# Four edits to a six-stage decoder kernel: product order in two fp8 attention stages, seven groups in the shared expert, and the last feed-forward's input built a block earlier

## The chip, the cores and the metric

The kernel runs on one core of one Trainium2 chip. The metric is the device time of one execution in microseconds (us); the number given for a kernel is the median over several executions. The engines are named as in the profile: PE (TensorE, matrix products), PEld (its weight loads), DVE (VectorE), ACT (ScalarE), POOL (GpSimd) and SP (SyncE, which issues most transfers). Each works through its own queue in order, and instructions wait on one another through semaphores.

## The reference

The reference is a pre-norm decoder of two layers over x of shape (16, 112, 512), that is 1792 tokens in 14 tiles of 128, with a context of shape (16, 375, 512). All is in f32 except where values are rounded to fp8. Six residual steps follow one another:

```
x = x + L0_attn(layernorm(x))                 # causal self attention, 16 heads of 32
x = x + L0_xattn(layernorm(x), ctx)           # fp8 self attention and fp8 cross attention, one output projection
x = x + L0_ffn(layernorm(x))                  # mixture of 8 experts, top 2, and a shared expert
x = x + L1_attn(layernorm(x))                 # causal self attention with biases
x = x + L1_xattn(layernorm(x), ctx)           # cross attention of one wide head
x = x + L1_ffn(layernorm(x))                  # SwiGLU with ternary weights, 512 -> 2048 -> 512
```

The parts that the change touches:

```
# L0_xattn: rows are scaled, clipped, rounded to bf16 and then to fp8; 16 query heads, 8 key heads of 128
q = _ln(linear(ln_out, wq), qln)      k = _ln(linear(ln_out, wk), kln)     v = linear(ln_out, wv)
kx, vx = split(cond @ w_kv_x.T)       kx = _ln(kx, kxln)
cat = concat(gqa(q, k, v), gqa(qx, kx, vx))
out = linear(fp8(cat / proj_smooth), wproj)
# L0_ffn, the shared expert, hidden size 448
out = silu(xf @ sw1) * (xf @ sw3) @ sw2
# L1_ffn
out = (silu(x @ wu.T) * (x @ wg.T)) @ wd.T
```

## The kernel before

The residual x stays on chip as 14 tiles of 128 tokens. The stages run one after another: first attention (to about 262 us of the span), fp8 self attention (262 to 900), fp8 cross attention (900 to 2247), the mixture of experts (2247 to 2786), the second layer's attention (2786 to 3104), its cross attention (3104 to 3458) and its feed-forward (3458 to the end).

**fp8 self attention.** `stage_fp8_self` works on four quarters of the heads (q = 0 to 3) times 16 batches. The list `order` holds these units; quarters 0 and 1 are interleaved, since quarter 0 waits for its inputs. The function `turn(n)` issues, in a fixed order, the pieces of several units at different depths: the projection of queries of unit n (`project_q`), the scores of unit n-2, the keys and values of unit n (`project_kv`, `ps_kv`), the values of unit n-3, the normalization of unit n (`normalize`, tile `qk`), the transposes of unit n-1, and the output of unit n-4. PE and ACT run in the order written; from turn 5 on DVE does too. POOL and SP, and DVE in turns -2 to 4, are ordered by the scheduler.

Units of quarter 0 that bring a new tile have a `Quantized` input: `load` fetches a normed row tile `xn`, `transpose` writes `ps_xt` on PE, `scale(count)` makes the bf16 tiles `y` on ACT from it (10 pieces in one turn, 6 in the next), `round_qk` rounds to fp8 for queries and keys (tile `xq`: four passes on DVE in `round_fp8`, then a subtraction on POOL), and `round_v` does so for values (tile `xv`). In the kernel before, an input for unit n is loaded at the end of turn n-3, transposed and scaled in turn n-2, and rounded in turn n-1, `round_v` near its end. Between them PE also runs 16 `early` products (`ps_early`, L697), one for each batch: the keys and values of the last third of the context for the first cross quarter, stored to DRAM. The dictionary `early` says how many stand at the start of each turn.

**fp8 cross attention.** `stage_fp8_cross` has again four quarters times 16 batches. A `CrossUnit` projects queries (`queries`, tile `qn`), then keys and values in three chunks of 125 context rows (`keys_values(ch)`, L1135, tiles `kn`, with one buffer, and `vn`). In the first quarter the third chunk needs no product: its result was made early and is loaded. Each chunk is normed at once by `normed`: squares on ACT, a sum on DVE (`cu_v`, L1111), an inverse root on POOL (L530, L531), a multiplication on DVE (L1113). `scores` computes the scores of two heads, their maximum (`ex_m`, L1078) and exponentials (L1079), the reciprocal, and the division of the probabilities (`pr`, L1170). `transpose_probs` (L1178), `values` (L1188) and `output` (L708, then x on DVE, L948) follow. In turn n the units n, n-1 and n-2 are mixed, and the scheduler orders the engines by that program.

**Shared expert.** In the mixture of experts, `shared_expert` returns a list of steps for a block of 4 or 3 tiles (512 or 384 tokens): four `up(f)`, each with two groups of four f32 products over 112 of the 448 hidden columns (L1444), a silu on ACT (L1447) and a product on DVE (`h`, L1448), and one `down(i)` per tile (L1455), four products each. Blocks 0 and 1 are computed around the routing of the tokens, blocks 2 and 3 at the end of the stage, beside the gathers of the experts' rows on POOL (`yg`, L1420), and ACT's reading of the feed-forward's weights (`w_sum`, L1776). An f32 product stands as two instructions in the trace.

**Last feed-forward.** `stage_ffn` goes through four blocks of 4, 4, 3 and 3 tiles. For each it takes the layer norm, transposes the rows (`ps_xt`, L1823) and splits them into two parts (`halves`, tile `xt`, L1804 on ACT and L1805 on DVE), and then runs 16 steps over the hidden columns, each with `ps_u` and `ps_g` (L1854) and the `down` of the step before (`ps_o`, L1836). `ps_u` and `ps_xt` share two banks.

Of the kernel before, what the change touches and what calls it, by code (L numbers as in the profile page):

```python
# [2 lines left out]

# [6 lines left out]
F32 = mybir.dt.float32  # L10
# [20 lines left out]
TILE_BLOCKS = ((0, 4), (4, 4), (8, 3), (11, 3))  # L31
E, HID = 8, 448
HC = 112
MOE_WIDTHS = (KC * HID, KC * HID, 4 * D)
MT = (2 * B * S + E * (P - 1)) // P
FQ = 4
# [927 lines left out]
def stage_fp8_self(k):  # L964
# [4 lines left out]
    with k.stage("s2a", mm=3, tr=1, sc=4) as wk:  # L969
# [36 lines left out]
        end = max(inputs)  # L1006

        def turn(n):
            new, half = inputs.get(n + 2), inputs.get(n + 1)
            products(early.get(n, 0))  # L1010
            if at(n):
                units[n].project_q(weights[order[n][0]], xq.pop(n))
            if at(n - 2):
                units[n - 2].scores()
            if at(n):
                units[n].query_sums()
            if half:
# [24 lines left out]
            if n >= last[1] and tiles and not loaded:  # L1042
                loaded.append((tiles[0], cross_input(k, wk, tiles.pop(0))))
            if at(n - 1):
                units[n - 1].transpose()
            if new:
                new.transpose()
                new.scale(10)
            elif at(n + 2):
# [32 lines left out]
class CrossUnit:  # L1082
# [3 lines left out]
    def __init__(self, k, wk, q, b, w, heads):  # L1086
        self.k, self.wk, self.q, self.b, self.w = k, wk, q, b, w
        self.heads, self.tile = heads, tile_of(b)
        if self.tile is not None:
            self.xq = wk.tile([P, KC, P], F32R, tag="xq", name="xq", bufs=2)  # L1090
            k.nc.sync.dma_start(out=self.xq.bitcast(F32), in_=k.xx_dram[self.tile])
        self.ct = ct = wk.tile([P, KC * SC + 12], F32, tag="ct", name="ct", bufs=2)
        if q == 0:
            n = SC - CC
            self.ct, self.early = chunks(ct, 0, KC, n), ct[:CC, KC * n :].rearrange(
                "p (h d) -> p h d", d=P
            )
            k.nc.sync.dma_start(out=self.ct, in_=k.a["ctx_t"][b][:, :, :n])
            k.last_load = k.nc.sync.dma_start(out=self.early, in_=k.kv_dram[b])
        else:  # L1100
            self.ct = chunks(ct, 0, KC, SC)
            k.last_load = k.nc.sync.dma_start(out=self.ct, in_=k.a["ctx_t"][b])
# [21 lines left out]
    def keys_values(self, ch):  # L1124
        k, wk, nc = self.k, self.wk, self.k.nc
        w = chunks(self.w.kv, 0, KC, 512)
        if ch == 0:
            self.kn = wk.tile([CC, NCH, 2, P], F32, tag="kn", name="kn", bufs=1)
            self.vn = wk.tile([CC, NCH, 2, P], F32, tag="vn", name="vn", bufs=2)
        if ch == NCH - 1 and self.q == 0:  # L1130
            pkv = self.early
        else:
            pkv = k.psum.tile([CC, 4, P], F32, tag="mm", name="ps_kv", bufs=3)
            for c in range(KC):
                nc.tensor.matmul(  # L1135
                    pkv, self.ct[:, c, ch * CC : (ch + 1) * CC], w[:, c, :],
                    start=c == 0, stop=c == KC - 1,
                )
# [17 lines left out]
    def scores(self, heads):  # L1156
# [10 lines left out]
        nc.vector.reciprocal(sums, sums)  # L1167
        for i, h in enumerate(heads):
            pr = self.pr[:, h, :]
            nc.vector.tensor_scalar(pr, pr, sums[:, i : i + 1], None, ALU.mult)  # L1170

    def transpose_probs(self):
        k, wk, nc = self.k, self.wk, self.k.nc
# [23 lines left out]
            add_output(self.k, t, self.heads.o.pop(t), self.w.get(1), "acc")  # L1197


def stage_fp8_cross(k):  # L1200


    with k.stage("s2b", mm=3, tr=2, sc=2, acc=1) as wk:
        units = []
        for n in range(4 * B + 2):
            q, b = divmod(n, B)
            new = last = None
            if q < 4:
                if b == 0:
                    w, heads = k.next_w, Heads()  # L1210
                new = CrossUnit(k, wk, q, b, w, heads)
                units.append(new)
                new.queries()
                new.keys_values(0)
            if 0 < n <= 4 * B:
                last = units[n - 1]
                last.scores((0, 1))
            if new:
                new.keys_values(1)
            if last:  # L1220
                last.scores((2, 3))
            if new:
                new.keys_values(2)

            first = new is None or q == 0
            if n > 1 and first:
# [12 lines left out]
                k.next_w.step(1)  # L1239
            if b == 2 and q == 3:  # L1240
                with behind(k):
                    k.weights["shared"] = load_pieces(k, "shared", k.a["shared_w"], MOE_WIDTHS)


def gates(k, wk, gw, xts):
# [185 lines left out]
def shared_expert(k, wk, xt, first, count):  # L1431

    nc, n = k.nc, count * P
    w1, w3, w2 = moe_weights(k.weights["shared"])
    tok = slice(first * P, first * P + n)
    hs = []

    def up(f):
        cols = slice(f * HC, (f + 1) * HC)
        p1 = k.psum.tile([HC, n], F32, tag="sc", name="ps_1", bufs=2)  # L1440
        p3 = k.psum.tile([HC, n], F32, tag="mm", name="ps_3", bufs=3)
        for pp, w in ((p1, w1), (p3, w3)):
            for c in range(KC):
                nc.tensor.matmul(pp, w[:, c, cols], xt[:, c, tok], start=c == 0, stop=c == 3)  # L1444
        sl = wk.tile([P, 4 * P], F32, tag="sl", name="sl", bufs=2)[:HC, :n]
        h = wk.tile([P, 4 * P], F32, tag="h", name="h", bufs=5)[:HC, :n]
        nc.scalar.activation(sl, p1, AF.Silu)  # L1447
        nc.vector.tensor_tensor(h, sl, p3, ALU.mult)  # L1448
        hs.append(h)

    def down(i):
        x = k.x[:, first + i, :]
        po = k.psum.tile([P, D], F32, tag="mm", name="ps_o", bufs=3)
        for f in range(4):
            nc.tensor.matmul(  # L1455
                po, hs[f][:, i * P : (i + 1) * P], w2[:, f, :], start=f == 0, stop=f == 3
            )
        nc.vector.tensor_tensor(x, x, po, ALU.add)

# [345 lines left out]
    k.nc.vector.tensor_tensor(lo, x, hi.bitcast(F32), ALU.subtract)  # L1805


def stage_ffn(k):
    nc, t = k.nc, k.ternary
    rows_out = k.out.rearrange("b s d -> (b s) d")  # L1810
    with k.stage("s6", mm=3, tr=2, sc=2, acc=1) as wk:
        todo = [(q, m) for q in (2, 3) for m in range(3)]
        for first, count in TILE_BLOCKS:
            nt = count * P
            rows = [k.x[:, first + i, :] for i in range(count)]
            xt = wk.tile([P, 2, KC, 4 * P], F32R, tag="xt", name="xt", bufs=2)[:, :, :, :nt]
            mv, rs = row_stats(k, rows)
            for i, r in enumerate(rows):
                xn = wk.tile([P, D], F32, tag="xn", name="xn", bufs=2)
                normalize(k, xn, r, mv, rs, i)  # L1820
                ps = k.psum.tile([P, KC, P], F32, tag="sc", name="ps_xt", bufs=2)
                for c in range(KC):
                    nc.tensor.transpose(ps[:, c, :], xn[:, c * P : (c + 1) * P], k.ident)  # L1823
                tok = slice(i * P, (i + 1) * P)
                halves(k, xt[:, 0, :, tok], xt[:, 1, :, tok], ps)
# [15 lines left out]
            for n in range(4 * FQ):  # L1841
# [93 lines left out]
def laid_out(i):  # L1935
# [70 lines left out]
    got["shared_w"] = expert_w(sw1, sw3, sw2)  # L2006
# [20 lines left out]
```

## Time and profile before

| what | us |
|---|---|
| median of 3 runs | 3805.27 (3802.48 to 3808.19) |
| the profiled execution | 3800.22 |
| its span | 3798.5 |
| PE busy in it | 3600.9 (95%) |
| DVE, ACT, POOL busy | 1785.3, 1429.4, 927.7 |
| mean granted PE clock | 0.983 |

All lines of the profile come from the one profiled execution, so sums over its rows are to be set against 3800.22, not against the median. The span leaves out 1.7 us around the program. A row of the timeline gives start, length, engine, line, operation and tiles, and in brackets the idle time just before it with what ended that. The granted clock is the rate that the PE had; at 0.5 a product takes about double.

### The profile page before, as it was taken

The page shows a single profiled execution, that of the slowest core. Times are in us where ns is not written, and L with a number is a line of the kernel's source. Part 1 is how long each engine was busy: PE and PEld are TensorE (multiplying, and loading weights), DVE is VectorE, ACT ScalarE, POOL GpSimd, SP SyncE. Part 2 cuts the span into 40 slices and gives each one's busy share as a digit, 9 for nine tenths or more (in the row PEclk, how much of TensorE's full clock was granted, in tenths as well). Part 3 has the DMA queues.
Part 4 walks back from the last instruction along what each step waited for, and adds up shares of the span by engine and source line. Part 5 has one row for each costly group of instructions (what it writes and reads, how often), then busy time and mean ns, then how long its engine had stood idle before and what let it go on. Part 6 is the DMA issues. An engine that isn't in the chain of part 4 may idle for free.

```text
span 3798.5 us, 46330 instructions
## 1 busy us (share of the span) xinstructions
PE 3600.9 (95%) x16482; PEld 2325.5 (61%) x16482; DVE 1785.3 (47%) x3888; ACT 1429.4 (38%) x4133; POOL 927.7 (24%) x1314
## 2 busy tenths in 40 slices
PE   7988899998999999999999999999989999999999
PEld 4545787886555566566666654555544445556788
DVE  5546777876445544544445542111243453224333
ACT  3546766554444444444444430111124431112222
POOL 2324555653222322322222210000132220000000
PEclk9999999999999999999999999999989999999999
DMA  2144333432211211211121114999830022222000
GB/s 84 58 140 142 114 111 122 151 118 73 62 55 63 66 50 47 74 47 52 44 82 44 49 40 145 319 318 317 297 117 12 1 78 76 74 80 76 12 12 17
DMA packets 118118, 364.56 MB, mean 96 GB/s; under 512 B 13280, under 2 KB 33248, under 8 KB 108848
## 3 DMA queue, kind: packets, MB, share of 16 engines
q1 hardware_dynamic: 105504, 332.20, 27.0%
q0 software_dynamic: 5040, 16.52, 1.2%
q10 hardware_dynamic: 7344, 12.89, 0.9%
q8 instruction: 131, 2.15, 0.2%
q14 instruction: 99, 0.81, 0.1%
HBM read 317.09 MB, written 44.47 MB: 95 GB/s over the span
## 4 chain that ended last, share of the span: by engine, by line
PE 69%; DVE 10%; POOL 5%; issue 3%; ACT 2%; DMA 2%; POOLq 0%; SPq 0%; ACTq 0%; DVEq 0%
PE ps_kv L1135 14%; PE ps L1492 6%; PE ps_av L1188 4%; PE ps_s L1163 3%; PE ps_y L1510 3%; PE ps_acc L708 3%; PE ps_q L708 3%; PE ps_u L1854 3%; PE ps_o L360 3%; PE ps_o L1836 3%; PE ps_g L1854 3%; PE ps_q L1605 3%; PE ps_p L1698 3%; PE ps_pt L1178 2%; PE ps_v L1620 1%
## 5 line engine op out<-in xcount | busy, mean ns | idle before, releaser
L1135 PE MATMUL ps_kv<-w_kv,ct 128*125 128x512 f32 x1408 | 637.6, 592 | 0.0
L1135 PEld LDWEIGHTS ps_kv<-w_kv,ct 128*125 128x125 f32 x1408 | 260.2, 187 | 276.1 <-issue 242.0
L549 POOL TENSOR_TENSOR r_o<-r_t,r_m 128x64 fp32r<-128x64 bf16 (+6 forms) x224 | 146.4, 670 | 331.4 <-DVE r_t L547 307.7
L1111 DVE TENSOR_REDUCE cu_v<-sq 125x2 f32<-125x256 f32 (+1 forms) x248 | 118.6, 478 | 215.7 <-ACT sq L1110 215.7
L1079 ACT ACTIVATE pr<-ps_s,ex_m 112x375 f32<-112x375 f32 (+1 forms) x272 | 157.4, 579 | 165.3 <-DVE ex_m L1078 154.9
L1492 PE MATMUL ps<-w_expert,xgt 128*128 128x448 f32 x560 | 216.4, 539 | 0.7 <-ACT xgt L1484 0.7
L530 POOL TENSOR_SCALAR cu_v<-cu_v 125x2 f32<-125x2 f32 (+1 forms) x248 | 48.0, 194 | 635.5 <-DVE cu_v L1111 633.2
L531 POOL TENSOR_TENSOR cu_v<-cu_v,mhalf 125x2 f32<-125x2 f32 (+1 forms) x248 | 190.0, 766 | 20.4
L236 POOL TENSOR_TENSOR pr<-pr,nq_s 112x448 f32<-112x448 f32 (+1 forms) x120 | 118.5, 988 | 296.1 <-DVE nq_s L235 243.7
L231 ACT ACTIVATE pr<-ps_s,nq_m 112x112 f32<-112x112 f32 (+1 forms) x480 | 166.9, 378 | 60.6 <-DVE nq_m L223 59.6
L1163 PE MATMUL ps_s<-kt,qt 128*112 128x375 f32 x512 | 183.6, 479 | 1.9 <-ACT pr L1079 1.4
L1078 DVE TENSOR_REDUCE ex_m<-ps_s 112x1 f32<-112x375 f32 (+1 forms) x272 | 148.1, 545 | 69.3 <-PE ps_s L1725 67.0
L1110 ACT ACTIVATE sq<-ps_kv 125x256 f32<-125x256 f32 x176 | 67.4, 383 | 272.4 <-PE ps_kv L1135 218.3
L524 ACT ACTIVATE qt<-ps_t,turned 128x448 f32<-128x448 f32 (+6 forms) x224 | 116.4, 581 | 131.3 <-PE ps_t L1147 122.5
L1188 PE MATMUL ps_av<-pt,vn 125*128 125x224 f32 x768 | 164.1, 363 | 0.0
L1492 PEld LDWEIGHTS ps<-w_expert,xgt 128*128 128x128 f32 x560 | 103.6, 190 | 92.0 <-issue 91.0
L1178 PEld LDWEIGHTS ps_pt<-ident,pr 112*125 112x125 f32 x768 | 104.0, 190 | 86.9 <-DVE pr L1170 49.1
L1188 PEld LDWEIGHTS ps_av<-pt,vn 125*128 125x128 f32 x768 | 146.3, 195 | 9.5 <-ACT pt L1181 4.6
L1163 PEld LDWEIGHTS ps_s<-kt,qt 128*112 128x112 f32 x512 | 89.9, 177 | 101.2 <-issue 59.3
L1178 PE MATMUL ps_pt<-ident,pr 112*125 112x112 f32 x768 | 119.2, 284 | 32.0 <-DVE pr L1170 29.8
L524 ACT ACTIVATE kt<-ps_t,vec 128x375 f32<-128x375 f32 (+7 forms) x240 | 131.3, 587 | 26.4 <-PE ps_t L1153 22.6
L1113 DVE TENSOR_TENSOR kn<-ps_kv,cu_v 125x256 f32<-125x256 f32 x176 | 74.7, 424 | 136.9 <-POOL cu_v L531 133.9
(298 smaller groups left out, 7346.1 us busy)
## 6 DMA issues: line engine op xcount, KB each, us to landing
w_expert<-in_moe_w SPq DMA_DIRECT2D x105, 896.0 KB
ct<-in_ctx_t SPq DMA_DIRECT2D x64, 750.0 KB
xq<-xq_dram SPq DMA_DIRECT2D x42, 512.0 KB
xq<-xx_dram SPq DMA_DIRECT2D x56, 256.0 KB
raw<-in_self_w SPq DMA_DIRECT2D x48, 256.0 KB
w_sum<-in_ffn_w SPq DMA_DIRECT2D x12, 1024.0 KB
cn<-in_ctx SPq DMA_DIRECT2D x16, 750.0 KB
xv<-xv_dram SPq DMA_DIRECT2D x48, 224.0 KB
```

The costliest lines, as they stand in the source:

```text
L231: nc.scalar.activation(pr[:, j, :], self.ps[:, j, r * t : (r + 1) * t], AF.Exp, bias=self.mx[r][:, j : j + 1], scale=-1.0, accum_out=sums[ ...
L524: k.nc.scalar.activation(dst, src, AF.Identity, bias=cols[:, 1:2], scale=cols[:, 0:1])
L531: nc.gpsimd.tensor_tensor(dst, dst, bc(k.minus_half[: dst.shape[0]], [dst.shape[0], n]), ALU.pow)
L708: k.nc.tensor.matmul(out, lhs(c), w[i][:, c, :], start=first and c == 0 and i == 0, stop=last and c == n - 1 and i == 1,)
L1078: nc.vector.tensor_reduce(mx, src, AX.X, ALU.min)
L1079: nc.scalar.activation(dst, src, AF.Exp, bias=mx, scale=-1.0, accum_out=sums)
L1135: nc.tensor.matmul(pkv, self.ct[:, c, ch * CC : (ch + 1) * CC], w[:, c, :], start=c == 0, stop=c == KC - 1,)
L1163: nc.tensor.matmul(ps, self.heads.qt[self.b][:, h, :], self.kt[:, h // 2, :], start=True, stop=True)
L1178: nc.tensor.transpose(ps[:, h, :], self.pr[:, h, ch * CC : (ch + 1) * CC], k.ident[:S, :S])
L1188: nc.tensor.matmul(av[:, 2 * g : 2 * g + 2, :], self.vn[:, ch, g, :], self.pt[:, ch, 2 * g : 2 * g + 2, :], start=ch == 0, stop=ch == NCH - 1,
L1492: nc.tensor.matmul(pp, self.xt[:, c, :], w[:, c, :], start=c == 0, stop=c == 3)
L1854: nc.tensor.matmul(pp, w[:, c, cols], xt[:, part, c, :], start=c == 0 and part == 0, stop=c == 3 and part == 1,)
```

## The change

There are four edits; the attentions of the second layer aren't touched.

1. In `stage_fp8_self`, each entry of `early` becomes a pair: so many products at the start of the turn, and so many behind the transposes of unit n-1, ahead of those of the new input. They are spread from turn -2 to turn 5. Inputs of units behind the first unit of quarter 1 (units 10, 12, 15, 17, 19 and 22; `apart` in the code) are loaded, transposed and scaled one turn earlier and rounded for queries and keys two turns ahead; `round_v` stays one turn ahead, but stands at the start of the turn.
2. In the first quarter of `stage_fp8_cross`, the early chunk is normed first, ahead of the queries. The norms of the other two chunks are issued behind the divisions of the last unit's scores (0, 1) and (2, 3), by `behind_division`. The other quarters keep their order.
3. The shared expert's up products go in groups of 128 hidden columns: three for each of the two matrices, and one in which the last 64 columns of both stand side by side, seven groups for eight. Silu of that last group reads rows 0 to 63 and writes rows 64 to 127. The weights are packed to match.
4. In `stage_ffn`, `FfnInput` holds the norm and the transposes of a block as steps. The next block's are issued in the last steps of the block before, one tile per step, ahead of `down`; the first block's at its start, as before.

```diff
-        early = {-2: 4, -1: 1, 0: 2, 1: 2, 2: 3, 3: 2, 4: 2}
+        early = {-2: (4, 0), -1: (1, 0), 0: (1, 1), 1: (1, 1), 2: (1, 1), 3: (1, 1), 4: (1, 0), 5: (2, 0)}
+        begun, rounded, rounded_v = {}, {}, {}
+        for n, put in inputs.items():
+            apart = n > order.index((1, 0))
+            begun[n - 2 - apart], rounded[n - 1 - apart], rounded_v[n - 1] = put, (n, put), (apart, put)
...
-            new, half = inputs.get(n + 2), inputs.get(n + 1)
-            products(early.get(n, 0))
+            new, (to, half) = begun.get(n), rounded.get(n, (None, None))
+            apart, half_v = rounded_v.get(n, (None, None))
+            products(early.get(n, (0, 0))[0])
...
+            if apart:
+                half_v.round_v()
             if half:
                 half.round_qk()
-                xq[n + 1] = half.xq
+                xq[to] = half.xq
...
-            if half:
-                half.round_v()
+            if half_v and not apart:
+                half_v.round_v()
...
                 units[n - 1].transpose()
+            products(early.get(n, (0, 0))[1])
             if new:
                 new.transpose()
                 new.scale(10)
...
-            if n + 3 in inputs:
-                inputs[n + 3].load()
+            if n + 1 in begun:
+                begun[n + 1].load()
...
-        self.normed(self.kn[:, ch], pkv[:, 0:2, :])
-        nc.scalar.copy(self.vn[:, ch], pkv[:, 2:4, :])
+        def norm():
+            self.normed(self.kn[:, ch], pkv[:, 0:2, :])
+            nc.scalar.copy(self.vn[:, ch], pkv[:, 2:4, :])
+
+        return norm
...
+def behind_division(k, unit):
+    return k.tc.issue_after(unit.division.ins) if unit else nullcontext()
...
+                steps = [2, 0, 1] if q == 0 else [0, 1, 2]
+                if q == 0:
+                    new.keys_values(steps.pop(0))()
                 new.queries()
-                new.keys_values(0)
+                norm = new.keys_values(steps.pop(0))
+                if q:
+                    norm()
             if 0 < n <= 4 * B:
                 last = units[n - 1]
                 last.scores((0, 1))
+
             if new:
-                new.keys_values(1)
+                if q == 0:
+                    with behind_division(k, last):
+                        norm()
+                norm = new.keys_values(steps.pop(0))
+                if q:
+                    norm()
             if last:
                 last.scores((2, 3))
-            if new:
-                new.keys_values(2)
+            if new and q == 0:
+                with behind_division(k, last):
+                    norm()
+            if new and steps:
+                new.keys_values(steps.pop(0))()
...
     def up(f):
...
+        sl = wk.tile([P, 4 * P], F32, tag="sl", name="sl", bufs=2)[:, :n]
+        h = wk.tile([P, 4 * P], F32, tag="h", name="h", bufs=5)[:, :n]
+        if f < 3:
+            cols, rows = slice(f * P, (f + 1) * P), slice(0, P)
+            p1, p3 = product(w1[:, :, cols], "sc", 2), product(w3[:, :, cols], "mm", 3)
+        else:
+            rows = slice(64, P)
+            p3 = product(both, "sc", 2)
+            p1 = p3[:64]
+        nc.scalar.activation(sl[rows], p1, AF.Silu)
+        nc.vector.tensor_tensor(h[rows], sl[rows], p3[rows], ALU.mult)
+        hs.append(h[rows])
...
+class FfnInput:
+    def __init__(self, k, wk, first, count):
+        self.k, self.wk, self.first, self.count = k, wk, first, count
+        self.rows = [k.x[:, first + i, :] for i in range(count)]
+        self.steps = [self.begin] + [lambda i=i: self.transpose(i) for i in range(count)]
+
+    def begin(self):
+        shape = [P, 2, KC, 4 * P]
+        xt = self.wk.tile(shape, F32R, tag="xt", name="xt", bufs=2)
+        self.xt = xt[:, :, :, : self.count * P]
+        self.mv, self.rs = row_stats(self.k, self.rows)
+
+    def transpose(self, i):
+        k = self.k
+        xn = self.wk.tile([P, D], F32, tag="xn", name="xn", bufs=2)
+        normalize(k, xn, self.rows[i], self.mv, self.rs, i)
+        ps = k.psum.tile([P, KC, P], F32, tag="sc", name="ps_xt", bufs=2)
+        for c in range(KC):
+            k.nc.tensor.transpose(ps[:, c, :], xn[:, c * P : (c + 1) * P], k.ident)
+        tok = slice(i * P, (i + 1) * P)
+        halves(k, self.xt[:, 0, :, tok], self.xt[:, 1, :, tok], ps)
...
+                if 4 * FQ - 1 - n <= len(ahead) and ahead:
+                    ahead.pop(0)()
+
                 if n > 0:
                     down(n - 1, then)
```

More of the change, by code (lines that the diff above doesn't have):

```diff
@@ L1 @@
 import math
-from contextlib import ExitStack, contextmanager
+from contextlib import ExitStack, contextmanager, nullcontext
 import concourse.bass as bass
@@ L33 @@
 HC = 112
+SHARED_WIDTHS = (KC * (HID + P - 64), KC * (HID - 64), 4 * D)
 MOE_WIDTHS = (KC * HID, KC * HID, 4 * D)
@@ L1048, in turn @@
                 new.scale(10)
-            elif at(n + 2):
+            if at(n + 2) and n + 2 not in inputs:
                 q, b = order[n + 2]
@@ L1088, in __init__ @@
         self.heads, self.tile = heads, tile_of(b)
+        self.kn = None
         if self.tile is not None:
@@ L1126, in keys_values @@
         w = chunks(self.w.kv, 0, KC, 512)
-        if ch == 0:
+        if self.kn is None:
             self.kn = wk.tile([CC, NCH, 2, P], F32, tag="kn", name="kn", bufs=1)
@@ L1169, in scores @@
             pr = self.pr[:, h, :]
-            nc.vector.tensor_scalar(pr, pr, sums[:, i : i + 1], None, ALU.mult)
+            self.division = nc.vector.tensor_scalar(pr, pr, sums[:, i : i + 1], None, ALU.mult)
     def transpose_probs(self):
@@ L1241, in stage_fp8_cross @@
                 with behind(k):
-                    k.weights["shared"] = load_pieces(k, "shared", k.a["shared_w"], MOE_WIDTHS)
+                    k.weights["shared"] = load_pieces(
+                        k, "shared", k.a["shared_w"], SHARED_WIDTHS
+                    )
 def gates(k, wk, gw, xts):
@@ L1433, in shared_expert, with product @@
     nc, n = k.nc, count * P
-    w1, w3, w2 = moe_weights(k.weights["shared"])
+    pieces = k.weights["shared"]
+    w1, w3 = (chunks(p, 0, KC, HID - 64) for p in pieces[:2])
+    both, w2 = chunks(pieces[0], KC * (HID - 64), KC, P), chunks(pieces[2], 0, 4, D)
     tok = slice(first * P, first * P + n)
     hs = []
-    def up(f):
[L1439 to L1449, printed above, removed]
+    def product(w, tag, bufs):
+        ps = k.psum.tile([P, n], F32, tag=tag, name="ps", bufs=bufs)
+        for c in range(KC):
+            nc.tensor.matmul(ps, w[:, c], xt[:, c, tok], start=c == 0, stop=c == 3)
+        return ps
+    def up(f):
+        sl = wk.tile([P, 4 * P], F32, tag="sl", name="sl", bufs=2)[:, :n]
[10 more added lines that the diff above has]
+        hs.append(h[rows])
     def down(i):
@@ L1455, in down @@
             nc.tensor.matmul(
-                po, hs[f][:, i * P : (i + 1) * P], w2[:, f, :], start=f == 0, stop=f == 3
+                po, hs[f][:, i * P : (i + 1) * P], w2[64:, f, :] if f == 3 else w2[:, f, :],
+                start=f == 0, stop=f == 3,
             )
@@ L1805, in halves @@
     k.nc.vector.tensor_tensor(lo, x, hi.bitcast(F32), ALU.subtract)
+class FfnInput:
[13 more added lines that the diff above has]
+        ps = k.psum.tile([P, KC, P], F32, tag="sc", name="ps_xt", bufs=2)
+        for c in range(KC):
+            k.nc.tensor.transpose(ps[:, c, :], xn[:, c * P : (c + 1) * P], k.ident)
+        tok = slice(i * P, (i + 1) * P)
+        halves(k, self.xt[:, 0, :, tok], self.xt[:, 1, :, tok], ps)
 def stage_ffn(k):
@@ L1812, in stage_ffn @@
         todo = [(q, m) for q in (2, 3) for m in range(3)]
-        for first, count in TILE_BLOCKS:
-            nt = count * P
[L1815 to L1825, printed above, removed]
+        inputs = [FfnInput(k, wk, *block) for block in TILE_BLOCKS]
+        for this, after in zip(inputs, inputs[1:] + [None]):
+            while this.steps:
+                this.steps.pop(0)()
+            first, count, rows, xt = this.first, this.count, this.rows, this.xt
+            nt = count * P
+            ahead = after.steps if after else []
             out = [
@@ L2005, in laid_out @@
     got["L0_ffn_gate_w"] = i["L0_ffn_gate_w"]
-    got["shared_w"] = expert_w(sw1, sw3, sw2)
+    sw1, sw3 = kxm(sw1.T).reshape(P, KC, HID), kxm(sw3.T).reshape(P, KC, HID)
+    sw2 = np.concatenate([sw2[: HID - 64], np.zeros((64, D), np.float32), sw2[HID - 64 :]])
+    got["shared_w"] = pack(
+        sw1[:, :, : HID - 64], np.concatenate([sw1[:, :, HID - 64 :], sw3[:, :, HID - 64 :]], 2),
+        sw3[:, :, : HID - 64], sw2.reshape(4, P, D).transpose(1, 0, 2),
+    )
     got["moe_w"] = np.stack([expert_w(w1[e], w3[e], w2[e]) for e in range(E)])
```

## The prediction

> **What bounds the kernel now.** I read the busy shares and the chain first, then a table of stretches, then the waits of TensorE (PE) in the stretches that the change touches, then their rows.
>
> ```profile
> PE 3600.9 (95%) x16482; PEld 2325.5 (61%) x16482; DVE 1785.3 (47%) x3888; ACT 1429.4 (38%) x4133; POOL 927.7 (24%) x1314
> PE 69%; DVE 10%; POOL 5%; issue 3%; ACT 2%; DMA 2%; POOLq 0%; SPq 0%; ACTq 0%; DVEq 0%
> ```
>
> PE is the bound: only fewer PE instructions or fewer PE gaps can move the end. The columns below are stretch, length, busy time by engine, granted PE clock, DMA share and GB/s.
>
> ```profile
> 262.00:530.00 268.00, 233.25 (x1233) 181.47 (x1232) 181.99 (x382) 178.77 (x559) 129.92 (x142) 0.94 0.39 129
> 964.00:1242.00 278.00, 258.86 (x1025) 162.11 (x1023) 142.05 (x357) 125.16 (x307) 70.93 (x136) 1.00 0.19 58
> 2236.00:2353.00 117.00, 111.19 (x371) 55.48 (x369) 42.27 (x123) 18.55 (x30) 7.78 (x15) 0.97 0.33 112
> 3458.00:3798.50 340.50, 324.62 (x1528) 276.43 (x1528) 130.44 (x187) 86.05 (x143) 2.09 (x2) 0.99 0.07 26
> ```
>
> PE misses 34.8, 19.1, 5.8 and 15.9 us in the four: first self turns, first cross quarter, first shared blocks, last FFN. The waits of the first two (line waited for: total, times, longest):
>
> ```profile
> PE ps_s L875 <- ACT kt L524: 9.1, 4, 4.2
> PE ps_kv L708 <- POOL xv L549: 8.1, 6, 1.9
> PE ps_kv L708 <- DVE qk L853: 4.9, 2, 3.7
> PE ps_xt L154 <- ACT y L739: 4.8, 5, 2.2
> PE ps_q L708 <- POOL xq L549: 3.5, 3, 1.4
> ...
> PE ps_pt L1178 <- DVE pr L1170: 18.7, 14, 2.7
> ```
>
> **Cross quarter (964 to 1242).** Nearly every turn of 20.1 us has one wait: transposes of the probabilities stand behind the second division. The chain of one turn:
>
> ```profile
> 1074.76 3.45 PE ps_kv L1135 x8
> 1078.57 0.39 ACT sq L1110
> 1078.99 0.43 DVE cu_v L1111
> 1079.77 0.71 POOL cu_v L531
> 1080.84 0.54 DVE ex_m L1078
> 1081.38 0.34 DVE cu_v L1111
> 1082.07 0.70 POOL cu_v L531
> 1082.80 0.42 DVE kn L1113
> 1083.30 0.65 DVE x L948
> 1084.33 0.47 PE ps_pt L1178 x2
> ```
>
> The chunk's norm (sum, POOL's rsqrt, kn) stands on DVE ahead of the division, which lands at about 1084.3, 6.1 us after the product ends. The new DVE order is two ex_m, reciprocal, two divisions, then cu_v, x, kn. From the product's end: scores 1.26, but ex_m queues behind the first chunk's kn until about 1.5; two ex_m 1.1; last exponential and its sum 0.7; reciprocal 0.16; first division 0.37: about 3.9 us, at 1082.1. PE now reaches the waiting transposes earlier, since only the output product (1.85) and six transposes (about 0.85) stand ahead: 1082.0. A wait of 0.1 to 0.3 is left of 1.65. The 14 waits sum to 18.7; the last, 2.7, is at the boundary to the next quarter, which keeps its order. Of the other 16.0 I leave 13 x 0.25: **-12.5 us**. Ends: 0 (the wait comes back as below) and -16.0. The norm's own new delay, about 2 us, is covered, as are ACT's square and copy of vn (0.4 each), which move with it: kn is first transposed after the values' products (2.46), at about 1088.9, against kn at about 1085.4. Without that cover it would cost what it exceeds.
>
> **Self stage (262 to 530).** Sixteen early products (3.44 us each: sixteen instructions in 7.03 us are two) are spread later. Two effects. (a) Turn 0 has one product fewer ahead of its query projection, so the wait for xq at 287.60 grows from 1.42 to about 4.9. The second product now stands ahead of the input transposes and covers their five waits for y (4.8). Adding up the rows, by the projection of turn 5 PE is about 1.4 us late, but has then run all sixteen products, the last two at the start of turn 5; while they run, the chains behind the earlier units go on, and so they cover the 1.15 wait for kt and the 3.72 for qk, so its key product comes at about 357, not 360.89: **-4**. The 4.19 and 3.38 waits for kt behind it (DVE centers weights just ahead) move along and stay. Bounds: +3.5 (only the new wait) and -8. (b) Later inputs are rounded one turn earlier. Of the 8.1 us for xv, 1.95 belongs to an input that isn't moved: 6.15 go; of the xq waits, 1.09 and 1.03: **-8**. The moved work is POOL's 2.13 (xq) and 1.29 (xv), four DVE passes each, ACT's scalings, the load of xn and the stores on SP's queue; SP's issues take 0.26 to 0.45 each and wait for nothing here. POOL's xv now precedes xq and the turn's rsqrt (1.5 us), and would delay qk by at most its own 1.29 in six turns: +8 at worst, which would make (b) nothing; each was in the same turn behind that rsqrt before. Sum **-12**, ends +5 and -20.
>
> A rule on the clock is weighed here. Rows: half clock for 6.83 us followed the 3.72 wait (from 358.76, key product 2.07 instead of 1.17) and also a 2.69 wait (from 1242.81); it did not follow the 2.35 at 276.31 nor the cross waits up to 1.65. So I count the stretch that goes with the 3.72 wait (-3.4 at most) against the one that a 4.9 wait may bring: nothing net. The stretch at 423.61 follows waits of 1.47 or less and may go: up to -3.4, left in the range. The Trainium skill, "TensorE: Matmul & The Clock Gate", section "HAM oscillation", names idle gaps above about 3.4 us as what halves the clock. By it the new 4.9 wait speaks against this change (+3.4), the 3.72 pays it back, and the stretch at 423.61 could not be gained; the trace's half clock after 2.69 us disagrees, so the row decides.
>
> **Shared expert.** Seven groups of four products for eight. The rows, by group, wait of PE in block 0, and block 3:
>
> ```profile
> L1444 PE MATMUL ps<-xts,w_shared 128*112 128x512 f32 x128 | 57.4, 595 | 0.0
> ```
>
> ```profile
> 2287.48 2.74 PE L1444 MATMUL ps<-xts,w_shared 128*112 128x512 f32 x6
> 2290.52 2.00 PE L1409 MATMUL ps_tab<-g_what,place 128*128 128x70 f32 x16 [0.30 <-DVE g_what L1399]
> ```
>
> Eight instructions take 3.44 us, so each of blocks 0 and 1 loses 3.44 of PE work. Block 0's cover the routing chain on DVE, whose g_what (2290.46) PE then meets earlier: the 0.30 grows by about 2, so -1.5. Block 1 is dense PE work: -3.4. Blocks 2 and 3 (2.58 each) end with the gathers and with ACT's silu, which is queued behind w_sum's DMA (PE already waits 5.01 there): 0. **-5**; ends -1 and -12. A 128x512 operation over 64 rows is costed like one over 112. The pieces of the weights' load change size, not their sum, and land long before (PE starts on them at 2253 without a wait).
>
> **FFN.** Each of three block boundaries has this (3555 shown):
>
> ```profile
> 3555.54 1.03 PE L1823 MATMUL ps_xt<-ident,xn 128*128 128x128 f32 x8
> 3557.93 1.23 PE L1823 MATMUL ps_xt<-ident,xn 128*128 128x128 f32 x8 [1.35 <-DVE xt L1805]
> 3559.83 0.73 PE L1854 MATMUL ps_g<-xt,w_ffn 128*128 128x512 f32 x2 [0.68 <-ACT xt L1804]
> ```
>
> The transposes move into the last steps of the block before, four at a time ahead of a down product of 1.9 us; the work stays, the waits (2.03, 2.40, 1.98) go: **-6.4**. The cover: their eviction (ACT 0.6, DVE 0.65) beside DVE at 130 of 340 us. Had PE to wait for the evicted bank at each of ten rows, 0.7 each, it would be +0.6.
>
> Sum: -12.5 - 12 - 5 - 6.4 = -35.9 against the profiled run, 3800.22 (span 3798.5 and 1.7 around it): 3764.3. That run is 5.05 below the median of 3805.27, so on the median's scale **3769 us**.
>
> **The rivals.**
> 1. Cross waits move: the early chunk's kn (one buffer) now stands on DVE ahead of the queries' norm and of ex_m, and waits for the last unit's transposes. For it: kn, query sum, rsqrt and qn (0.42, 0.68, 0.9, 0.73) must pass between those transposes (until about 1091.0) and the first scores (1094.2), which is nearly all of the 3.2 us. Against: 1 us of slack in the second half. Gain lost: about -23.5, 3782.
> 2. The self stage gains nothing, by the 4.9 wait, a half clock of 3.4 and POOL's order: -24, 3781.
> 3. Slower: the mechanism of 1, larger. If that norm chain ends late by more than the slack, every division does, in 16 turns. The other parts give 23.4, so beyond 1.5 us more per turn than before (23.4/16) the whole is slower; at 2.5 us, 40 - 23.4 = +16.6: 3822. Against it: no such wait in the rows, where all of these operations are short.
> 4. The change does nothing that counts: each wait's end is set by something just behind it, and only block 1's -3.4 is left: 3802. For it: PE is busy for 95% of the span, so each gain is a short wait with other work right behind it. Against: in the cross quarter the chain above has one end, and it is shortened.
>
> **How the numbers follow.** About 0.2% (7.6 us) is what can be told from no change. Forecast 0.65; rival 1 0.11; 2 0.11; 4 0.06; 3 0.07. Faster 0.87, same 0.06, slower 0.07. The forecast alone runs from 3754 (cross -16, self -20, the clock's -3.4, the rest as summed) to 3777 (cross and self 4 short each); the range takes in rivals 1 and 2 and half of 4: 3750 to 3796.
>
> **What would show it.** Cross: the waits for the division fall from 18.7 to under 6 and PE's gaps in 964 to 1242 from 19 to about 7; wrong, if ps_s or ps_t waits appear instead. Self: one wait of about 4.9 on xq near 287, none on qk near 357, and under 3 us on xv. Shared: 112 up products for each pair of blocks by shape instead of 128, and a longer wait on g_what. FFN: no wait on xt at three boundaries. The prediction is wrong if the self stage's first 22 turns take as long as before, or if the queries' norm holds ex_m.

## The result, and the profile after

The changed kernel takes 3751.11 us (median of 4 executions, 3748.44 to 3755.31), the kernel before 3806.73 beside it (4 executions). The ratio is 0.986, 95% interval 0.983 to 0.990: 1.4% faster. It was measured twice more, on two different chips (runs e5 and e12 below), at 0.988 (0.986 to 0.989) and 0.988 (0.985 to 0.991): 46.4 and 42.7 us. The forecast was 3769, range 3750 to 3796. All three medians (3751, 3753 and 3755) lie in the range, near its low end; the first two lie below the 3754 to 3777 that the forecast alone was to cover.

The profiled execution of the changed kernel took 3748.44 us, its span 3746.7, which is 51.8 below that of before. The opening lines and the chain of the page after:

```profile
PE 3581.0 (96%) x16450; PEld 2315.4 (62%) x16450; DVE 1799.2 (48%) x3888; ACT 1426.2 (38%) x4133; POOL 928.7 (25%) x1314
PE 69%; DVE 9%; POOL 5%; ACT 3%; issue 3%; DMA 1%; POOLq 0%; SPq 0%; ACTq 0%; DVEq 0%
```

PE is still the bound. It is busy for 19.9 us less, and its gaps are 31.9 us shorter; these are the two halves of the 51.8. Below are the same five stretches of work in both, cut at the first PE instruction of each stage (length, then busy time and instructions by engine, granted clock, DMA share, GB/s). Before: fp8 self stage, first cross quarter, the other three, shared blocks 0 and 1, last feed-forward.

```profile
258.40:899.20 640.80, 577.84 (x3409) 483.70 (x3408) 478.00 (x1024) 387.13 (x1250) 331.61 (x384) 0.97 0.38 124
899.20:1203.40 304.20, 279.42 (x1097) 174.48 (x1097) 153.44 (x382) 140.22 (x343) 86.79 (x159) 0.99 0.22 66
1203.40:2251.90 1048.50, 1032.12 (x3882) 639.40 (x3880) 520.16 (x1239) 449.11 (x1071) 260.08 (x489) 0.99 0.16 53
2251.90:2353.10 101.20, 100.23 (x326) 47.04 (x325) 35.56 (x106) 15.55 (x25) 4.81 (x5) 1.00 0.35 118
3464.20:3798.50 334.30, 321.43 (x1512) 274.19 (x1512) 124.48 (x177) 83.81 (x139) 2.09 (x2) 0.99 0.07 24
```

After:

```profile
258.10:888.40 630.30, 572.38 (x3409) 481.33 (x3408) 481.30 (x1025) 388.47 (x1252) 332.26 (x386) 0.97 0.39 126
888.40:1173.60 285.20, 279.24 (x1097) 175.33 (x1096) 164.59 (x384) 135.67 (x341) 87.66 (x156) 0.99 0.22 70
1173.60:2218.90 1045.30, 1029.44 (x3882) 637.40 (x3881) 520.25 (x1236) 449.37 (x1070) 261.82 (x491) 0.99 0.16 54
2218.90:2316.20 97.30, 96.34 (x309) 44.54 (x308) 35.25 (x106) 15.46 (x25) 4.73 (x5) 1.00 0.37 123
3421.60:3746.70 325.10, 318.88 (x1512) 273.87 (x1512) 123.37 (x177) 83.15 (x139) 2.08 (x2) 0.99 0.07 25
```

The first cross quarter gives 19.0 us with PE's work as it was (279.4 and 279.2): all of it is waiting. The self stage gives 10.5, the shared blocks 3.9, nearly all of it PE work (100.23 to 96.34), the feed-forward 9.2. The other three quarters give 3.2 though nothing in them changed, as does the second cross attention (2.6), while the second attention loses 1.7. The last part of the expert stage, which holds the shared blocks 2 and 3, gives 4.8; whether the change does that is taken up below.

The waits of PE after, from 276 to 530 us (the first fence), and in the first cross quarter (the second fence: before, then after):

```profile
PE ps_s L876 <- ACT kt L525: 11.2, 4, 5.8
PE ps_kv L709 <- DVE qk L854: 6.1, 5, 3.0
PE ps_xt L155 <- ACT y L740: 5.7, 2, 3.4
PE ps_q L709 <- POOL xq L550: 3.7, 2, 3.2
PE ps_acc L709 <- ACT pr L889: 1.7, 1, 1.7
PE ps_av L908 <- ACT pt L902: 1.1, 2, 0.7
```

```profile
PE ps_pt L1178 <- DVE pr L1170: 22.9, 17, 3.1
PE ps_pt L1195 <- DVE pr L1187: 4.3, 15, 0.9
```

The wait for xv, 8.1 us before, is gone, with the 1.95 of an input that isn't moved. The waits for kt, qk and y, 18.8 before, are 23.0; 2.36 of this stood before at the same place as a wait for xn. In the cross quarter, whose waits for the division were 22.9 in the same stretch, 4.3 are left.

### The profile page after: what moved, and what is told of

The parts are those of the page before. It is cut to its first block, busy times and chain, and to the rows that moved or that the text cites. A ratio compares the mean times of both kernels' runs of the same rounds, so it can differ in the third digit from the quotient of the medians.

```text
span 3746.7 us, 46264 instructions
## 1 busy us (share of the span) xinstructions
PE 3581.0 (96%) x16450; PEld 2315.4 (62%) x16450; DVE 1799.2 (48%) x3888; ACT 1426.2 (38%) x4133; POOL 928.7 (25%) x1314
## 3 DMA queue, kind: packets, MB, share of 16 engines
q8 instruction: 131, 2.15, 0.2%
## 4 chain that ended last, share of the span: by engine, by line
PE 69%; DVE 9%; POOL 5%; ACT 3%; issue 3%; DMA 1%; POOLq 0%; SPq 0%; ACTq 0%; DVEq 0%
PE ps_kv L1148 14%; PE ps L1542 6%; PE ps_av L1205 4%; PE ps_s L1180 3%; PE ps_y L1560 3%; PE ps_q L709 3%; PE ps_acc L709 3%; PE ps_u L1924 3%; PE ps_o L361 3%; PE ps_o L1906 3%; PE ps_g L1924 3%; PE ps_q L1655 3%; PE ps_p L1748 3%; PE ps_pt L1195 2%; PE ps_v L1670 1%
## 5 line engine op out<-in xcount | busy, mean ns | idle before, releaser
L532 POOL TENSOR_TENSOR cu_v<-cu_v,mhalf 125x2 f32<-125x2 f32 (+1 forms) x248 | 190.3, 767 | 20.5
L709 PE MATMUL ps_acc<-w_cross,r_o 128*128 128x512 f32 x448 | 134.6, 428 | 3.7 <-POOL r_o L550 3.7
```

The lines of the kernel that those rows point to most:

```text
L532: nc.gpsimd.tensor_tensor(dst, dst, bc(k.minus_half[: dst.shape[0]], [dst.shape[0], n]), ALU.pow)
L709: k.nc.tensor.matmul(out, lhs(c), w[i][:, c, :], start=first and c == 0 and i == 0, stop=last and c == n - 1 and i == 1,)
```

## The experiments

Stage lengths in what follows are taken from each run's own profiled execution, cut at the same instructions as above, and set against the profile of before. The profiles of kernels in which a stage is unchanged show how far it moves by itself: the self stage by +0.8 to -3.6, the first cross quarter by +1.2 to -0.7, the other quarters by -0.2 to -3.3, the end of the expert stage by +3.7 to -3.2, the second cross attention by -0.3 to -6.3, and the last feed-forward by +1.0 to +3.1 (in the profile of before it is the shortest of all unchanged ones). The first two shared blocks, where the clock stayed at 1.00, never moved by 0.1. Differences below these are not read.

**Each edit alone.** The kernel before with one edit, three rounds each, on one chip.

```diff
# e1: only stage_fp8_self     e2: only CrossUnit and stage_fp8_cross
# e3: only shared_expert, SHARED_WIDTHS and the weights' packing     e4: only FfnInput and stage_ffn
```

> Only the new product order and the earlier roundings of the fp8 self stage. If each edit pays in its own stage, as the two profiles side by side suggest, the self stage ends about 10.5 us earlier, the rest keeps its length within 4 us (the clock's phase), and the whole is faster by 8 to 13 us. If the profile's gain there was a lucky phase of the clock, under 6 us.

> Only the new order of norms in the first cross quarter. By the two profiles the first quarter ends 19 us earlier; the other quarters' 3.3 us are two shorter stretches at half clock. Theory: faster by 18 to 23 us, waits of the probabilities' transposes for the division under 7 us in all (25 with the first rounds). Rival (my working): 12.5 us, since a wait of 0.25 stays in each turn.

> Only the seven groups of the shared expert. My working: 5 us, all of it in blocks 0 and 1. Theory from the two profiles: 8.5 us, 3.7 of it in blocks 0 and 1 and 4.8 in blocks 2 and 3, where the gathers wait for additions on DVE that stand behind the fourth h. If the 4.8 came from the phase of the transfers, this run gives 3 to 5 us.

> Only the feed-forward's input built a block earlier. My working: 6.4 us, the waits alone. Theory from the two profiles: 9.2 us, about 3 at each of three boundaries, since PE's work at the boundary goes too (4.3 us from the last down product to the first gate product) and only 0.44 us per tile comes back in the steps.

| edit alone | median, us (before 3798.3) | ratio, interval | own stage, us |
|---|---|---|---|
| self stage | 3786.61 | 0.997 (0.995 to 1.000) | -7.6 |
| cross quarter | 3780.97 | 0.995 (0.993 to 0.998) | -18.3 |
| shared expert | 3796.30 | 1.000 (0.998 to 1.001) | -3.8 |
| feed-forward | 3788.93 | 0.999 (0.997 to 1.001) | -9.2 |

Each edit pays in its own stage, and by the same amount alone as together, within what the stage moves by itself. By the medians only the cross quarter's interval excludes 1; what the other three are worth rests on their stages. The medians sum to 40.4, the own stages to 38.9. The end of the expert stage moved by -1.5 with the shared edit alone, and by -0.9 to -4.8 in four profiles of kernels that have it with the others (the changed one three times, and e8; that of e11, which was disturbed there, is left out); kernels without it moved between +3.7 and -3.2. The theory that the edit gains 4.8 there fell: though PE has 16 instructions fewer there, the gain can't be told from nothing, which is what the prediction had.

**All four, and two more edits.** The changed kernel on the same chip as its relatives, five rounds, and with two of its leftover waits attacked.

```diff
 # e8, on the changed kernel
-        early = {-2: (4, 0), -1: (1, 0), 0: (1, 1), 1: (1, 1),
+        early = {-2: (4, 0), -1: (2, 0), 0: (1, 1), 1: (1, 0),
...
-                if q == 0:
+                if q == 0 or b == 0:
                     with behind_division(k, last):
                         norm()
```

> The changed kernel itself, beside its relatives on one chip. Theory (each edit pays in its own stage): its stages are shorter than the kernel before's by the same amounts as when the edits stand alone: first cross quarter 18 to 19, first shared blocks 3.8, last feed-forward 9.2, self stage 7 to 11; in all 45 to 55 us. Rival (edits help one another): the stages alone sum to about 40 and the rest shows as a stage that is shorter only here.

> The changed kernel with two more edits: two early products ahead of turn 0 instead of one (one fewer in turn 1), and the norms behind the divisions in the first turn of the other three quarters too. The first should remove the wait of 3.19 and its stretch at half clock (about 5 us, less up to 1 for an uncovered wait on y), the second about 1.5 of each of three waits of 2.7, 2.7 and 1.5 (4 us). Together 3 to 9 us faster than the changed kernel; 0 if POOL's centering of weights beside DVE at the boundary sets those divisions.

e5 took 3753.04 against 3799.47, 46.4 less. Its own stages are -9.1 (self), -18.2, -3.8 and -9.1, 40.2 together, of 45.3 between the profiles, so the other stages sum to -5.1; no stage is shorter only here by more than such a stage moves anyway. e8 took 3755.93, no faster than e5, where 3 to 9 us were expected. The wait for xq fell as expected, but the waits for y and for the division at the quarters' boundaries stood:

```profile
PE ps_pt L1195 <- DVE pr L1187: 6.9, 3, 2.7
```

That line of e8, from the other three quarters, is the same to the digit in e5 (6.9, 3, 2.7). It doesn't show what holds those divisions, because the edit missed their turns. In e8 the norm stands behind the division in the first turn of the second quarter (kn at 1182.60, the divisions from 1180.44), where no such wait was. The wait of 2.69, at 1212.88, comes one turn later, and there kn (1210.60) still stands ahead of the second maximum (1210.94). The third of the waits (1.46 at 2205.57) is in the last turn, which has no chunk to norm. Two other things stand ahead of the wait at 1212.88: DVE's centering of the next quarter's weights (`w_mean`, `raw`), and two divisions that take 2.76 us while POOL works on weights for 2.66, where such a pair takes 0.74 elsewhere. Which of the three holds it was not tested.

**The self stage in two halves.**

```diff
 # e6: only the new places of the early products; e11: the same in the changed kernel
-            apart = n > order.index((1, 0))
+            apart = False
 # e7: only the earlier inputs
-        early = {-2: (4, 0), -1: (1, 0), 0: (1, 1), 1: (1, 1), 2: (1, 1), 3: (1, 1), 4: (1, 0), 5: (2, 0)}
+        early = {-2: (4, 0), -1: (1, 0), 0: (2, 0), 1: (2, 0), 2: (3, 0), 3: (2, 0), 4: (2, 0)}
```

The lines marked - are those of the changed kernel's stage.

> From the kernel before, only the new places of the sixteen early products; no input is rounded earlier. My working: 4 us, with the wait for xq at turn 0 grown and the waits for y and qk (8.5 together) mostly gone, and the 8 us of waits for xv left. Rival: 0 or slower, since the wait at turn 0 brings a stretch at half clock (284.81, 6.83 us long, in the changed kernel's profile).

> From the kernel before, only the earlier load, scaling and rounding of six inputs; the early products stay where they were. My working: 8 us, waits for xv and xq from 11.6 to about 3.5. Rival: 0 to 4, since the waits for kt, qk and y that stand in the changed kernel (5.78, 2.95, 3.36, 2.98 near 365 to 408) come with the earlier roundings on DVE and POOL.

The products' new places alone: 3790.30 against 3799.47 (0.998, 0.997 to 1.000), self stage -11.2, more than either side expected. The earlier inputs alone: 3797.04 (1.000, 0.999 to 1.001), self stage +1.5. Here the rival was right. The waits of e7 from 276 to 530 us say why; those for xv and xq are gone, and the others have grown from 4.9 (qk), 4.8 (y) and 9.1 (kt):

```profile
PE ps_s L875 <- ACT kt L524: 10.6, 5, 3.8
PE ps_kv L708 <- DVE qk L853: 10.0, 7, 3.7
PE ps_xt L154 <- ACT y L739: 8.2, 6, 3.4
```

One turn shows the exchange. POOL's queue before, in the turn whose key product runs at 410.87 without a wait, and then in e7, where it waits 2.97:

```profile
404.11 0.93 POOL L893 TENSOR_TENSOR pr<-pr,su_s 112x448 f32<-112x448 f32 x1 [1.72 <-DVE su_s L892]
405.00 2.52 POOL L654 TENSOR_TENSOR w_self<-raw,w_self 128x512 fp32r<-128x512 f32 x2
407.49 0.23 POOL L530 TENSOR_SCALAR su_v<-su_v 128x6 f32<-128x6 f32 x1
407.80 1.42 POOL L531 TENSOR_TENSOR su_v<-su_v,mhalf 128x6 f32<-128x6 f32 x1
```

```profile
408.68 2.15 POOL L549 TENSOR_TENSOR xq<-r_t,r_m 128x1024 fp32r<-128x1024 bf16 x1
410.79 0.94 POOL L893 TENSOR_TENSOR pr<-pr,su_s 112x448 f32<-112x448 f32 x1
411.68 1.27 POOL L654 TENSOR_TENSOR w_self<-raw,w_self 128x512 fp32r<-128x512 f32 x1
412.91 0.23 POOL L530 TENSOR_SCALAR su_v<-su_v 128x6 f32<-128x6 f32 x1
413.22 1.34 POOL L531 TENSOR_TENSOR su_v<-su_v,mhalf 128x6 f32<-128x6 f32 x1
...
415.35 1.86 PE L708 MATMUL ps_kv<-w_self,xq 128*128 128x256 f32 x7 [2.97 <-DVE qk L853]
```

The rounding of xq, 2.15 us, has come into this turn and stands ahead of the probabilities and of the inverse root, on which qk waits. What PE no longer waits for at its inputs it waits for at its outputs.

> The changed kernel without the earlier load and rounding of the six inputs; all else as changed. Theory: the earlier rounding gains nothing, since POOL's rounding of xq (2.15 us) then stands ahead of the probabilities and the rsqrt of its turn, and waits for qk and y replace those for xv and xq. So 0 to 4 us faster than the changed kernel, self stage 10 to 12 us shorter than before's. Rival: the earlier rounding pays in the full change, and this is 4 to 8 us slower.

> The changed kernel beside the one without the earlier roundings, on the same chip: about 1.2% faster than before, and within 4 us of the other.

Without the earlier inputs the changed kernel took 3757.31 (0.988, 0.985 to 0.990), with them 3755.08 (0.988, 0.985 to 0.991): the same. The profile of e11 is of an execution at 3774.57, 17 us above its median. The excess stands in the expert stage (+9.4 in the experts, +7.1 at its end, against before). Its self stage is -6.5, where 10 to 12 were expected and where the changed kernel gives -9.1 to -10.8 in three profiles. By that the earlier inputs might be worth 2.6 to 4.3 us in the full change; e1 (-7.6) against e6 (-11.2) says the opposite, and both differences are within what the stage moves by itself. No version tried beats the changed kernel.

**The cross quarter in two halves.** One round each; the lines marked - are again those of the changed kernel.

```diff
 # e9: the early chunk first, no norm behind a division
-                if q == 0:
-                    with behind_division(k, last):
-                        norm()
+                if q == 0:
+                    norm()
 # e10: norms behind the divisions, the early chunk last as before
-                steps = [2, 0, 1] if q == 0 else [0, 1, 2]
+                steps = [0, 1, 2]
```

> From the kernel before, in the first cross quarter only the early chunk normed first; the norms of the other two chunks stay at once behind their products. The division then no longer stands behind the early chunk's sum, rsqrt and kn (1.4 us between the second maximum and the reciprocal), but the maxima still stand among the others' norms. If that norm alone makes the wait, the first quarter is shorter by 14 to 18 us of the 18.3 that both edits give; if the norms must all go behind the division, by 0 to 6.

> From the kernel before, only the norms of chunks 0 and 1 behind the divisions; the early chunk is normed last as before, by program order behind them. The division stands ahead of all norms. If the division alone counts, the first quarter is shorter by about 18 us here too; if the early chunk's norm at the end of the turn then makes kn late for its transposes, waits on kn appear and it is under 10.

First quarter: -15.3 with the early chunk first, -12.5 with the norms behind the divisions, -18.3 with both. The waits for the division in it are 10.2, 8.1 and 5.0. So either edit alone takes most of the gain, and they overlap. For e10 both expectations missed (about 18, or under 10). In it no wait on kn grew (1.3 as before), but eleven small ones on the transposed probabilities came (2.6 in all):

```profile
PE ps_pt L1183 <- DVE pr L1175: 8.1, 16, 2.2
PE ps_av L1193 <- ACT pt L1186: 2.6, 11, 0.2
PE ps_t L1158 <- DVE kn L1114: 1.3, 2, 0.8
```

## Why the prediction was right, and where its terms were not

The sum, -35.9, is against -46.4 and -42.7 in the two later comparisons, and -51.8 between the two profiles of the first. Of that 51.8, the four stretches that the terms are about hold 42.6, and the rest 9.2. That the sum came this close is in part luck: the cross quarter and the feed-forward gave 8.6 more than their terms, and the early products more than theirs, while the earlier inputs fell short by their whole 8 and the shared expert by 1.2.

**Cross quarter: -12.5 predicted, -18.3 measured alone; the mechanism was right, the term too small.** A turn's chain in the changed kernel, which answers to the one shown of before:

```profile
1055.62 0.20 POOL cu_v L531
1055.82 0.07 issue
1055.89 0.71 POOL cu_v L532
1056.62 0.44 DVE kn L1126
...
1058.05 1.12 ACT pr L1091 x4
1059.19 0.18 DVE cx_s L1184
1059.37 0.03 issue
1059.39 0.43 DVE pr L1187
1059.82 0.04 issue
1059.86 0.91 PE ps_pt L1195 x6
```

The division follows the exponentials directly, and the wait that is left is 0.17, where 0.1 to 0.3 were worked out and 0.25 taken (with 13 of these, 16.0 leaves 12.75, not 12.5). The missing part is the size of the window: the sum began at 964 us and left out the first rounds of the quarter, whose six waits over 0.3 between 899 and 964 us sum to 8.6 before (0.79, 0.52, 2.86, 0.77, 3.07, 0.55) and 3.1 after. With these 5.5 the step gives 18.0. The order of norms changed there too. Rivals 1 and 3, in which kn and the queries' norm come too late, did not occur: waits on kn are 0.8, less than before.

**Self stage: -12 predicted, -7.6 to -10.8 measured, but for the wrong reason.** Step (a), the products, was to give 4. Alone it gave 11.2 in e6, and 6.5 in e11, where the self stage is the same. Its mechanism was right, as the waits of e6 from 276 to 530 us show:

```profile
PE ps_s L875 <- ACT kt L524: 9.8, 3, 5.8
PE ps_kv L708 <- POOL xv L549: 8.1, 6, 1.9
...
PE ps_xt L154 <- ACT y L739: 2.4, 1, 2.4
...
PE ps_kv L708 <- DVE qk L853: 1.2, 1, 1.2
```

The five waits for y are covered (the 2.4 is the one that stood before as a wait for xn), and so is the 3.72 for qk. What the step had wrong is the query projection of turn 5, worked out as 1.4 us late; it is 3.2 us early in e6 (348.35 against 351.54), and the key product behind it comes at 351.73, not at about 357. The prediction's own rows make it early: a wait grown by 3.5 stands against 4.5 of covered waits for y (0.95, 0.27, 2.20 and 1.06). Besides, the wait at turn 0 was 3.38 in e6 and 3.19 in the changed kernel, rather than 4.9; over six profiles of kernels with these products it runs from 1.4 to 4.3. The wait for kt that was to stay, 4.19, grew to 5.78. Over the whole stage PE's gaps fell from 63.0 to 57.0 in e6 and 58.0 in e11. The rest went with less time at half clock: 30.7 us in e6 and 37.5 in e11, for 41.0 before, where the sum had nothing net.

Step (b), the earlier inputs, was to give 8 and gives nothing that can be measured. The waits that it named did go, and others came. Its own bound named the case in which it is worth nothing, but priced only POOL's 1.29 for xv and set it aside; the trace shows xq's 2.15, which stands in another unit's turn (POOL's order, which rival 2 had named). Two errors of opposite sign made a good sum.

On the clock, half rate for 6.83 us did come with the wait at turn 0 of the changed kernel's profile (from 284.81). The stretch that was to go with the 3.72 wait did not: one of 6.83 us stands from 366.73, where PE waits 5.78 for kt.

**Shared expert: -5 predicted, -3.8 measured; both halves of the working were off.** The first line is the down products of blocks 0 and 1 before. The others are of the changed kernel: the up products, then the down products over 128 and over 64 rows:

```profile
L1455 PE MATMUL ps_o<-w_shared,h 112*128 112x512 f32 x64 | 28.5, 595 | 0.0
...
L1482 PE MATMUL ps<-xts,w_shared 128*128 128x512 f32 x112 | 50.8, 597 | 0.0
L1504 PE MATMUL ps_o<-w_shared,h 128*128 128x512 f32 x48 | 22.7, 605 | 0.0
...
L1504 PE MATMUL ps_o<-w_shared,h 64*128 64x512 f32 x16 | 9.0, 641 | 0.0
```

The up products fell as forecast, from 57.4 to 50.8. Block 0 did not lose its share to the routing chain: the wait for g_what is 0.28 after and 0.30 before. But the down products, costed alike at any number of rows, rose from 28.5 to 31.7 (22.7 + 9.0). The step that failed is that one sentence; it is 3.2 us, nearly half of what the up products gained. Blocks 2 and 3 were costed at 0, which no run contradicts.

**Feed-forward: -6.4 predicted, -9.2 measured.** The boundary after:

```profile
3504.51 0.60 PE L1879 MATMUL ps_xt<-ident,xn 128*128 128x128 f32 x4
3504.86 2.11 PE L1906 MATMUL ps_o<-w_ffn,h 128*128 128x512 f32 x8
...
3510.49 4.12 PE L1906 MATMUL ps_o<-w_ffn,h 128*128 128x512 f32 x16
3514.45 1.80 PE L1924 MATMUL ps_u<-xt,w_ffn 128*128 128x512 f32 x7
```

No wait is left there, and the eviction is covered, as forecast. "The work stays, the waits go" counted only waits above 0.3. Before, 4.3 us passed from the end of the last down product (3555.54) to the first gate product (3559.83). From there to the second up product (3564.27) took another 4.4, where 3.7 is the pace of the steps. That is 5.0 lost. A step with a tile's transposes takes 5.98 instead of 5.54 to 5.60, so four give back 1.5 to 1.8. The net at this boundary is about 3.3, not 2.03. Over the stage PE's gaps fell by 6.6, which is the term, and its busy time by 2.6, which the term left out.

**The rest.** The other three quarters' -3.2 goes with the clock. Stretches at half rate in them fell from 20.5 to 13.7 us, and half of the 6.8 is 3.4; e1, with nothing changed in these quarters, shows the same -3.1 at 13.7. What moves the second cross attention and the end of the expert stage was not traced further; the cross attention moves as much between kernels in which it is the same, and the end of the expert stage between kernels without the shared edit.

## What to carry to other kernels

Where PE waits once per turn for an engine that serves two chains in order, first see which of the other chain's operations stand between the last input and the awaited result; moving either of them out was worth most of it here, and both together not twice. Filling PE's waits with independent products paid here (6.5 to 11.2 us), and making the inputs early did not, because the early inputs put their own roundings ahead of some other turn's results on an engine that works in order. Before an edit is said to leave a wait standing, see in the trace that the edit reached the turn in which the wait stands. Two price lines belong in such a sum: waits at the edges of a stage, and products of another height than their neighbours.

## What was not expected of the hardware

Products over 64 rows cost PE more than those over 112 or 128 when they stand between them. In the changed kernel's rows, f32 instructions of 512 columns over 128 rows start 0.429 us apart. The two over 64 rows and the changes to and from them are 0.52 to 0.53 apart, four such steps for each tile, or about 0.4 us; the eight tiles make up the 3.2 us above. The Trainium skill, "TensorEngine Tiling (Array Packing)", section "Key Properties", says that changing the tiling mode drains TensorE. The rows agree if a product over 64 rows counts as another mode; no run here tells a drain from a slower product of that height.

Stretches at half clock came in multiples of 3.41 us in every profile, but for the one at the program's end. Which waits brought one differed between executions of the same code: the wait for xq at turn 0 brought 6.83 us of it in one profile of the changed kernel (wait 3.19) and 3.41 in another (wait 4.29), and none in e6 (wait 3.38).
